# Pairwise products of 32 fields: cutting the first stores in fewer, larger pieces

One core of one Trainium2 chip; the metric is the device time of one execution in microseconds (us), median of several runs.

## The reference

```python
vid = jnp.einsum('bfd,de->bfe', x, W)          # x: (4096, 32, 64), W: (64, 64), float32
idx_i, idx_j = jnp.triu_indices(32, k=1)       # 496 pairs i < j
return x[:, idx_i, :] * vid[:, idx_j, :]       # (4096, 496, 64)
```

One small product with W, then 496 elementwise products per row of the batch. 34 MB come in and 520 MB go out: the output decides.

## The kernel before

The batch is cut into 16 tiles. In a tile the fields lie as `[128 partitions, field, 128]`, so a pair is 128 x 128 floats, 64 KB. TensorE makes `vid` in PSUM, VectorE multiplies into one of three output buffers of 124 pairs, SyncE issues the stores. From the third tile on there are four stores a tile, one of a whole buffer each (8.1 MB). In the first two tiles the buffers are sent in smaller pieces, so that the DMA engines have work before the first buffer is full; `GROWING` holds their sizes in pairs. The first two tiles of x are loaded on SyncE's queue, ahead of the stores; later ones on ScalarE's queue.

```python
GROWING = [21, 15, 19, 23, 27, 19, 29, ...]            # cut here: 26 sizes

loaded = [load(0, 4, nc.sync), load(1, 2, nc.sync)]    # 4 pieces, 2 pieces
...
for t in range(NT):
    if 0 < t < NT - 1:
        loaded.append(load(t + 1, 4, nc.scalar))
    ...                                                # matmuls of the tile
    for at, m, w, i, di, j, dj in products(by_field() if t < 2 else by_block()):
        base = at - at % SLOT                          # SLOT = 124
        if at == base:
            ot = opool.tile([P, SLOT, C], F32, tag="o", name=f"o_{t}_{at}")
        ...
        nc.vector.tensor_tensor(o, left, right, ALU.mult)
        at += n
        if t * NP + at == until or at in (base + SLOT, NP):
            nc.sync.dma_start(out=out[t][:, sent:at, :], in_=ot[:, sent - base : at - base, :])
            sent = at
            if t * NP + at == until:
                until += next(growing, NT * NP)
```

In the first two tiles the products come row by row: row j makes the j pairs (0, j) to (j-1, j). 21 pairs are the first six rows, 36 the first eight.

## Time and profile before

| | before |
|---|---|
| time, three runs | 1296.04 us (1294.44 to 1296.83) |
| profiled execution | 1297.8 us, span 1295.9 us |
| DMA engines | full in all of 40 slices but the last |
| VectorE busy | 1087.2 us, 84% |
| stores | 82, of them 26 cut by `GROWING` |

The lines are in the prediction below.

### The profile page before, as it was taken

Reading aid. Unit: us, or ns where it says so; the run is one execution under the profiler, and the core shown is the slowest. Engines: PE = TensorE matmul, PEld = TensorE weight load, DVE = VectorE, ACT = ScalarE, POOL = GpSimd, SP = SyncE. Lnnn points to the kernel's source line nnn. Section 1 sums busy time; section 2 is a strip of 40 time slices with the busy share of each in tenths; the row PEclk is TensorE's granted clock in tenths of the full one; section 3 lists DMA queues with packets and bytes.
Section 4 is the critical chain, followed back from the end, with each engine's and each line's share of the span. In section 5 each row is a group of like instructions: output and inputs, shape, how many; then the busy total and the mean of one; then the engine's idle time right before and its main releaser. Section 6 shows DMA issues by size and latency. Waiting matters only on the chain.

```text
span 1295.9 us, 1845 instructions
## 1 busy us (share of the span) xinstructions
PE 229.7 (18%) x512; PEld 48.5 (4%) x512; DVE 1087.2 (84%) x376; POOL 0.2 (0%) x4
## 2 busy tenths in 40 slices
PE   4112022112122121221212212122121221212000
PEld 1000000000000000000000000000000000000000
DVE  7999999788798887978879888798897978978870
POOL 0000000000000000000000000000000000000000
PEclk8555555555555555555655555555555555655555
DMA  9999999999999999999999999999999999999996
GB/s 390 431 422 439 427 431 450 432 423 439 430 434 429 425 438 434 424 432 429 435 432 432 433 433 433 434 432 433 435 432 432 431 432 432 430 431 445 437 425 276
DMA packets 20890, 553.80 MB, mean 427 GB/s; under 512 B 2448, under 2 KB 2448, under 8 KB 10256
## 3 DMA queue, kind: packets, MB, share of 16 engines
q1 hardware_dynamic: 12816, 524.33, 93.8%
q10 hardware_dynamic: 8064, 29.36, 5.5%
q8 instruction: 4, 0.07, 0.0%
q14 instruction: 6, 0.05, 0.0%
HBM read 33.59 MB, written 520.09 MB: 427 GB/s over the span
## 4 chain that ended last, share of the span: by engine, by line
DMA 55%; DVE 39%; issue 2%; PE 0%; DVEq 0%; SPq 0%
DMA out_dram<-o 55%; DVE o L159 39%; DMA x<-in_r_x_dram 0%; PE vid L134 0%; DVEq L200 0%; DVEq L159 0%; SPq L111 0%
## 5 line engine op out<-in xcount | busy, mean ns | idle before, releaser
L159 DVE TENSOR_TENSOR o<-x,vid 128x1024 f32<-128x1024 f32 (+15 forms) x376 | 1087.2, 2963 | 169.1 <-DMA out_dram<-o 124.3
L134 PE MATMUL vid<-x,w 64*64 64x512 f32 x512 | 229.7, 1032 | 958.6 <-DMA x<-in_r_x_dram 601.8
L134 PEld LDWEIGHTS vid<-x,w 64*64 64x64 f32 x512 | 48.5, 205 | 1138.1 <-DVE o L159 637.3
L182 POOL MEMSET const-uint8-127<- 128x1 uint8 x1 | 0.1, 103 | 0.0
L182 POOL MEMSET const-bfloat16-1.0<- 128x1 bf16 x1 | 0.1, 102 | 0.0
L182 POOL MEMSET const-float32-1.0<- 128x1 f32 x1 | 0.1, 100 | 0.0
L182 POOL MEMSET const-float32-0.0<- 128x1 f32 x1 | 0.1, 99 | 0.2 <-issue 0.2
## 6 DMA issues: line engine op xcount, KB each, us to landing
out_dram<-o SPq DMA_DIRECT2D x56, 7936.0 KB, 43.4
x<-in_r_x_dram ACTq DMA_DIRECT2D x56, 512.0 KB, 45.5
out_dram<-o SPq DMA_DIRECT2D x2, 3008.0 KB, 18.2
out_dram<-o SPq DMA_DIRECT2D x1, 5952.0 KB, 27.5
out_dram<-o SPq DMA_DIRECT2D x1, 4928.0 KB, 23.6
out_dram<-o SPq DMA_DIRECT2D x1, 4416.0 KB, 19.5
out_dram<-o SPq DMA_DIRECT2D x1, 4224.0 KB, 21.6
out_dram<-o SPq DMA_DIRECT2D x1, 3904.0 KB, 15.8
```

What stands on the lines that cost most here:

```text
L134: nc.tensor.matmul(vid[half, b : b + BANK, :], lhsT=w2[half, :], rhs=xt[half, b : b + BANK, :], start=True, stop=True,)
L159: nc.vector.tensor_tensor(o, left, right, ALU.mult)
L182: nc = _bacc.Bacc("TRN2", target_bir_lowering=False, num_devices=1, dynamic_dma_scratch_size=1024)
```

## The change

The intent is to issue the first store only when all first loads have landed, and to have fewer and larger stores behind it. Each further cut was chosen so that its store is ready before the stores ahead of it run out. Only the list changes.

```diff
 GROWING = [
-    21, 15, 19, 23, 27, 19, 29, 18, 19, 20, 38, 28, 24, 25, 47, 34, 29, 61,
-    55, 69, 66, 58, 77, 47, 93, 31,
+    36, 30, 25, 33, 29, 37, 41, 17, 52, 51, 21, 63, 61, 55, 69, 66, 58, 77,
+    47, 93, 31,
 ]
```

## The prediction

> **What bounds the kernel now.** I read the page first, from the span to the shares of the engines and the DMA rows.
>
> ```profile
> span 1295.9 us, 1845 instructions
> ...
> PE 229.7 (18%) x512; PEld 48.5 (4%) x512; DVE 1087.2 (84%) x376; POOL 0.2 (0%) x4
> ...
> DMA  9999999999999999999999999999999999999996
> ...
> q1 hardware_dynamic: 12816, 524.33, 93.8%
> q10 hardware_dynamic: 8064, 29.36, 5.5%
> ...
> HBM read 33.59 MB, written 520.09 MB: 427 GB/s over the span
> ```
>
> The DMA row is full in every slice but the last; VectorE, which makes the products, is idle for 16% of the span. The 16 DMA engines are the bound, and they are so from the first microseconds on. The reader should ask of any change here: does it take bytes away, does it make a byte cheaper, or does it open or close a hole in that row?
>
> Next I cut the span into stretches, to see the start, the growing stage, the steady part and the drain. The last two columns are the DMA share and the GB/s.
>
> ```profile
> 1.00:1.50 0.50, 0.00 (x0) 0.00 (x0) 0.00 (x0) 0.00 (x0) 1.00 0.00 0
> 1.50:2.00 0.50, 0.00 (x0) 0.00 (x0) 0.00 (x0) 0.00 (x0) 1.00 0.28 64
> ...
> 11.00:12.00 1.00, 1.00 (x8) 0.40 (x6) 1.00 (x2) 0.00 (x0) 1.00 1.05 442
> 12.00:13.00 1.00, 1.00 (x6) 0.30 (x4) 1.00 (x2) 0.00 (x0) 1.00 1.05 441
> 13.00:14.00 1.00, 1.00 (x8) 0.35 (x6) 1.00 (x1) 0.00 (x0) 1.00 0.98 414
> 14.00:15.00 1.00, 1.00 (x8) 0.25 (x4) 1.00 (x2) 0.00 (x0) 1.00 0.99 419
> 14.00:80.00 66.00, 12.34 (x32) 1.90 (x28) 66.00 (x33) 0.00 (x0) 0.56 1.02 431
> ...
> 300.00:1100.00 800.00, 145.56 (x314) 30.27 (x312) 673.09 (x215) 0.00 (x0) 0.53 1.00 432
> 1276.00:1280.00 4.00, 0.00 (x0) 0.00 (x0) 0.00 (x0) 0.00 (x0) 0.50 0.92 397
> 1280.00:1284.00 4.00, 0.00 (x0) 0.00 (x0) 0.00 (x0) 0.00 (x0) 0.50 0.62 270
> 1284.00:1288.00 4.00, 0.00 (x0) 0.00 (x0) 0.00 (x0) 0.00 (x0) 0.50 0.33 143
> 1288.00:1292.00 4.00, 0.00 (x0) 0.00 (x0) 0.00 (x0) 0.00 (x0) 0.50 0.04 16
> 1292.00:1296.00 4.00, 0.00 (x0) 0.00 (x0) 0.00 (x0) 0.00 (x0) 0.50 0.04 16
> ```
>
> Three things are to be seen. The hand-over from loads to stores (11 to 15 us) has no hole: 414 to 442 GB/s throughout. The growing stage (14 to 80 us) already runs at 431 GB/s against 432 in the steady part, so there is next to nothing to win in it. And the end is not a common one: the rate falls by steps for some 12 us, to 16 GB/s, less than one engine's share of 432/16 = 27. The last-finishing DMA engine sets the end; the others are done earlier. The whole then adds up: the full-rate body is 553.8 MB / 432 GB/s = 1282 us, the loss before the first packets is about 2.5 us, and the drain loses (4 us x 5) - (397+270+143+16+16) x 4 / 432 = 12.2 us; the sum, 1296.7, is the span to 1 us.
>
> Last, the queue that issues the stores, and the VectorE instruction that finishes pair 36 (start, length):
>
> ```profile
> 0.73 0.38 SPq L111 DMA_DIRECT2D w<-in_L_rec_W_dram  x1
> 1.17 3.12 SPq L117 DMA_DIRECT2D x<-in_r_x_dram  x6
> 10.89 0.35 SPq L162 DMA_DIRECT2D out_dram<-o  x1
> ...
> 13.02 0.34 SPq L162 DMA_DIRECT2D out_dram<-o  x1
> ...
> 11.78 1.22 DVE L159 TENSOR_TENSOR o<-x,vid 128x1024 f32<-128x1024 f32 x1
> ```
>
> The first store (21 pairs) is issued at 10.89, while the DMA engines still work through the loads. The second (up to pair 36) follows the eighth row of products, which ends at 11.78 + 1.22 = 13.00.
>
> **What the Trainium skill says.** Page "DMA: Bandwidth & Descriptors", section "Queues, rings and completion order": on each DMA engine the descriptors of one queue are consumed in ring order. First loads and stores share SyncE's queue, so a store issued before the loads are through is simply queued behind them and starts without a hole; the unbroken GB/s from 11 to 15 us agree. Same page, "Latency and other measured facts": about 600 ns to the first byte of a DMA issued by SyncE. The trace agrees if counted from the end of the issuing instruction: the issue of w ends at 0.73 + 0.38 = 1.11, nothing moves to 1.50, and in still finer stretches the first packets start between 1.70 and 1.80, some 0.63 us after it and 1.0 us after the issue began. Same page, "Anatomy of one DMA": a fixed cost of about 2 us per DMA, most of it the write receipt at completion. That would make five DMAs fewer worth 10 us if it lay on the path; the trace says it does not, since 431 GB/s with many small stores against 432 with large ones leaves at most 66 us x 1/432 = 0.15 us (rounding of the rates: up to 0.3) for all of the stores in that stage.
>
> **The change part by part.** It touches only where stores are cut: 26 sizes become 21, the first 36 instead of 21. Bytes, products, matmuls and their order are untouched; the built programs show 82 stores before and 77 after, and both lists meet again at pair 496 (the end of the first of 16 tiles), so everything from the second tile on is the same.
>
> Removed: five stores. In packets: each store is 128 rows and 16 completion packets, since (82 stores + 6 loads + 1 load of w) x 144 = 12816, the count of q1. So a store is 8 rows and one small packet per DMA engine. What a packet costs beyond its bytes I estimate from the two queue rows: q10 took 5.5% of 16 x 1295.9 us = 1140 us for 7168 packets of 4 KB, 159 ns each; q1 took 93.8% = 19449 us for 524.33 MB, 37.1 ns per KB, at a mean of some 46 KB per data packet. At q1's rate 4096 bytes would take 152 ns, so about 8 ns are left per packet, give or take 1.5 for the rounding of 5.5%. Per store 9 x 8 = 72 ns on each engine, all engines alongside; five stores: 0.36 us less.
>
> Added: a hole. The first store now waits for pair 36, so it is issued at 13.02, not 10.89; its first packets come 1.0 us later, about 14.05. When do the engines run out of loads? The six loads and w are 4.23 MB. From the rates of the first microseconds (about 3.4 MB moved by 10.9 us), 0.85 MB were left, or 2.0 us at 430 GB/s: 12.85 us in the mean, with some engines half a microsecond earlier and later. So each DMA engine idles 0.7 to 1.4 us, 1.15 in the mean, and since the DMA is the bound this is not earned back.
>
> Moved: the later stores. For no further hole, each must be issued 1.0 us before the stores ahead of it run out. One pair is 64 KB, 0.152 us at 430 GB/s, and the queue starts at 14.05. Store 2 (to pair 66) is ready when the eleventh row is, about 17.2, so its packets can come at 18.2; store 1 lasts to 14.05 + 36 x 0.152 = 19.5: 1.3 us to spare. The same sum for the others, with VectorE's times from the trace: to pair 91, 21.7 against 24.1; to 124, 26.3 against 27.9; to 153, 30.3 against 32.9; to 190, 35.4 against 37.3; to 231, 41.0 against 42.9; to 300, 50.4 against 51.8; to 351, 57.4 against 59.7; to 435, 68.8 against 70.6; to 496, 77.1 against 80.2. None is late, and a later start would only add room. VectorE's own pace, 0.133 us a pair and some 0.15 us an instruction, does not depend on the stores until its buffers come round again.
>
> Sum: +1.15 - 0.36 = +0.8 us, on 1296.04: 1296.8 us.
>
> **The rivals.** First, a gain: fewer, larger stores lift the growing stage by more than the packet sum. For it stands only the skill's fixed cost; against it the 431 GB/s. If the first store's early packets also disturbed the last loads, they would have to show as a dip at 11 to 13 us, and there is none. At its best this rival makes 1295.5 us. Second, a hidden hole: the last-finishing engine sets the end, and it might be one of those whose loads end late, so that its own hole is only 0.6 us; with the 0.36 saved the time is then 1296.3, the same as before. Third, a longer hole: the first loads needed until about 4 us to reach full rate after packets first moved at 2.2, so engines may start the store staggered. Stores read SBUF and not HBM, and w's packets all start within 0.3 us, which speaks against it; if it came, the hole would be near 2 us and the time 1297.8. Fourth, a new starvation at the tightest of the later stores (to pairs 66 and 300, 1.3 us to spare): each miss would add some tenths of a us, no more than 1 in all. Fifth, the drain: the spread of 12 us between DMA engines builds up over the long steady part, and a shift of the start may move it by a microsecond either way.
>
> **Range and chances.** The three runs of before spread over 2.4 us, more than the effect. From 1296.8, with a us for the drain and a us for the state of the run to both sides: 1294.8 to 1299.0. Two per cent would be 26 us; no part of this change touches even 3 us. Faster 0.005, within 2% 0.99, slower 0.005.
>
> **What would show it right or wrong.** In the changed kernel the one store issue at 13.02 must be the first; the stretch 13 to 14 us must fall far under 400 GB/s (to 100 or less) and 14 to 15 be full again; the stretch 15 to 80 should stay at 430 or more, which shows no later starvation; the steady part must keep 432, and the drain its 12 us. Wrong would be: no hole at 13 to 14 us (then a store starts faster than w did), a second hole later on, or a steady rate above 432, which would mean that the cuts of the first tile matter for the rest.

## The result, and the profile after

The changed kernel took 1301.14 us (median of 4 runs, 1300.61 to 1301.38), the kernel before, beside it, 1295.24 us (1293.92 to 1296.83). The ratio is 1.0044, with a 95% interval of 1.0027 to 1.0062; ratios here are the mean time of one kernel's runs over that of the other's of the same rounds, so not quite the ratio of the medians. It is outside the predicted range: 1296.8 us was said, 1299.0 at most.

The page of the changed kernel shows the same picture at its top, a little longer.

```profile
span 1298.7 us, 1833 instructions
...
PE 229.5 (18%) x512; PEld 48.6 (4%) x512; DVE 1087.3 (84%) x376; POOL 0.2 (0%) x4
...
q1 hardware_dynamic: 12096, 524.33, 93.5%
...
HBM read 33.59 MB, written 520.09 MB: 426 GB/s over the span
```

VectorE's work and all bytes are the same; q1 (SyncE's queue) has 720 packets fewer, which are the five stores at 144 packets. The stretches that the prediction asked for (columns: stretch and its length, busy time of the four engines, clock, DMA share, GB/s):

```profile
11.00:12.00 1.00, 1.00 (x6) 0.30 (x4) 1.00 (x2) 0.00 (x0) 1.00 1.06 451
12.00:13.00 1.00, 1.00 (x8) 0.43 (x6) 1.00 (x2) 0.00 (x0) 1.00 0.71 295
13.00:14.00 1.00, 1.00 (x8) 0.33 (x6) 1.00 (x2) 0.00 (x0) 1.00 0.02 8
14.00:15.00 1.00, 1.00 (x6) 0.30 (x4) 1.00 (x2) 0.00 (x0) 1.00 0.99 424
15.00:80.00 65.00, 12.42 (x32) 1.96 (x28) 65.00 (x32) 0.00 (x0) 0.54 1.02 432
...
300.00:1100.00 800.00, 146.38 (x318) 30.50 (x314) 674.17 (x217) 0.00 (x0) 0.53 1.00 433
1276.00:1280.00 4.00, 0.00 (x0) 0.00 (x0) 0.00 (x0) 0.00 (x0) 0.50 1.13 492
1280.00:1284.00 4.00, 0.00 (x0) 0.00 (x0) 0.00 (x0) 0.00 (x0) 0.50 0.84 365
1284.00:1288.00 4.00, 0.00 (x0) 0.00 (x0) 0.00 (x0) 0.00 (x0) 0.50 0.33 143
1288.00:1292.00 4.00, 0.00 (x0) 0.00 (x0) 0.00 (x0) 0.00 (x0) 0.50 0.07 32
1292.00:1296.00 4.00, 0.00 (x0) 0.00 (x0) 0.00 (x0) 0.00 (x0) 0.50 0.07 32
```

The hole is there, 8 GB/s from 13 to 14 us, and full rate right after it. No second hole follows (432 GB/s from 15 to 80 us), and the steady rate is unchanged. The first store and the row it waits for:

```profile
12.18 1.21 DVE L159 TENSOR_TENSOR o<-x,vid 128x1024 f32<-128x1024 f32 x1
...
13.42 0.35 SPq L162 DMA_DIRECT2D out_dram<-o  x1
```

It was issued at 13.42 and not at 13.02, since VectorE had waited longer for the matmuls: 0.62 us before its fourth row, against 0.23. That is scatter between executions and not the change: in a second trace of the kernel before the fourth row is late in the same way, and in neither trace of it does this open a hole.

So far the prediction holds. The two spans differ by 2.8 us; the medians of the timed runs by 5.9. The trace of before that I worked from was one of the slow executions of a kernel that scatters. What scatters is the drain, the time at the end in which one DMA engine after another runs out of work, and the trace lets us take it apart: each DMA engine closes its part of the last store with one packet of 4 bytes, so the start times of the last 16 such packets say when each of the 16 engines was done. This was worked out from the DMA packets of the traces (us after the first engine):

```
before, run of 1297.8 us: 0.0 0.0 0.1 0.2 0.2 0.2 0.3 0.3 1.8 2.1 3.2 5.1 6.6 7.1 7.2 12.5   first at 1282.20
before, run of 1291.9 us: 0.0 0.2 0.2 0.2 0.2 1.0 1.5 1.6 1.8 2.1 2.4 2.6 4.6 5.4 5.7  6.6   first at 1282.24
after,  run of 1300.6 us: 0.0 0.1 0.1 0.1 0.1 0.2 0.2 0.6 1.6 2.0 4.1 4.1 4.3 5.2 8.9 13.7   first at 1283.61
```

The mean engine of before is done at 1285.1 and 1284.5 us, that of after at 1286.4: a steady difference of some 1.6 us. The slowest is 9.6 and 4.3 us behind the mean before, and 10.9 after; this lag of the slowest engine, and its growth in the run, are called drift below. The kernel ends with the slowest. The question for the experiments was why the slowest engine falls so far behind after the change.

### The profile page after: what moved, and what is told of

Read it like the earlier page. It is cut to its first block, busy times and chain, and to the rows that moved or that the text cites. A ratio compares the mean times of both kernels' runs of the same rounds, so it can differ in the third digit from the quotient of the medians.

```text
span 1298.7 us, 1833 instructions
## 1 busy us (share of the span) xinstructions
PE 229.5 (18%) x512; PEld 48.6 (4%) x512; DVE 1087.3 (84%) x376; POOL 0.2 (0%) x4
## 4 chain that ended last, share of the span: by engine, by line
DMA 60%; DVE 36%; issue 1%; PE 0%; DVEq 0%; SPq 0%; ACTq 0%
DMA out_dram<-o 58%; DVE o L159 36%; DMA x<-in_r_x_dram 2%; PE vid L134 0%; DVEq L200 0%; DVEq L159 0%; SPq L111 0%; ACTq L117 0%; SPq L162 0%
```

## The experiments

Each batch ran on one chip with its own 11 runs of the kernel before; the kernels themselves ran six times, those of eight loads four and five; all results were correct. "Mean" is when the 16 DMA engines were done on average in the profiled execution, "behind" how much later the slowest was; the time of a run is the slowest engine's end plus 3.0 to 3.3 us.

| run | median us | range us | ratio to before | run traced | mean | behind |
|---|---|---|---|---|---|---|
| c_before | 1294.16 | 1291.92 to 1298.71 | 1.0000 | 1291.92 | 1284.5 | 4.3 |
| c_after | 1300.99 | 1300.29 to 1301.70 | 1.0045 | 1300.59 | 1286.5 | 10.8 |
| e_first36 | 1299.48 | 1299.16 to 1300.41 | 1.0035 | 1299.44 | 1286.3 | 10.1 |
| e_few_no_hole | 1295.95 | 1295.38 to 1296.65 | 1.0007 | 1295.91 | 1285.0 | 7.7 |
| e_first28 | 1300.47 | 1300.03 to 1301.11 | 1.0055 | 1300.74 | 1286.3 | 11.2 |
| e_first55 | 1301.78 | 1300.92 to 1302.68 | 1.0063 | 1302.68 | 1288.8 | 10.7 |
| e_late_hole | 1300.38 | 1299.96 to 1301.49 | 1.0045 | 1300.91 | 1287.3 | 10.6 |
| e_fill | 1298.83 | 1295.86 to 1301.17 | 1.0042 | 1295.86 | 1286.3 | 6.3 |
| e_fill_again | 1298.52 | 1296.61 to 1299.29 | 1.0027 | 1299.21 | 1286.8 | 9.2 |
| e_before_fill | 1300.38 | 1296.47 to 1300.65 | 1.0040 | 1298.93 | 1286.9 | 8.9 |
| e_before_stagger | 1294.36 | 1291.79 to 1297.78 | 0.9999 | 1294.09 | 1285.4 | 5.6 |
| e_stagger | 1300.51 | 1296.62 to 1302.47 | 1.0051 | 1301.88 | 1288.9 | 9.8 |
| e_oneq_before | 1298.65 | 1295.90 to 1302.55 | 1.0028 | 1299.25 | 1287.8 | 8.4 |
| e_oneq_after | 1301.82 | 1298.34 to 1303.11 | 1.0042 | 1298.34 | 1288.5 | 6.5 |
| e_oneq_first55 | 1305.13 | 1303.67 to 1307.25 | 1.0075 | 1307.25 | 1292.8 | 11.3 |
| e_load1 | 1303.34 | 1299.46 to 1308.25 | 1.0061 | 1303.69 | 1288.7 | 12.0 |
| e_load8_before | 1325.10 | 1324.90 to 1325.58 | 1.0235 | 1324.90 | 1320.7 | 1.2 |
| e_load8_after | 1322.85 | 1322.14 to 1325.57 | 1.0223 | 1322.85 | 1318.2 | 1.4 |

**Both kernels again.** No edit.

> The kernel before, unchanged, for a second trace and for the noise. Both theories: ratio 1.000 within 0.001, times of 1293 to 1298 us. The spread between the first and the last DMA engine at the end was some 12 us in the first trace, which was one of its slower executions (1297.8 us); if the drain explains the run-to-run range, a trace of a 1295 us execution should show some 3 us less of it.

> The changed kernel, unchanged, for a second trace. Again 1300.6 to 1301.4 us, ratio 1.0044. Theory 'hole': the engines idle some 1.5 us near 13 us and the rest of the 5.9 us is a longer drain. Theory 'chance': the time falls back to some 1297.5 us when it is run again.

The second trace of before caught a fast execution. Its drain (the same stretches; from 1280 us on):

```profile
1280.00:1284.00 4.00, 0.00 (x0) 0.00 (x0) 0.00 (x0) 0.00 (x0) 0.50 0.66 286
1284.00:1288.00 4.00, 0.00 (x0) 0.00 (x0) 0.00 (x0) 0.00 (x0) 0.50 0.18 79
1288.00:1292.00 4.00, 0.00 (x0) 0.00 (x0) 0.00 (x0) 0.00 (x0) 0.50 0.00 0
```

In the first trace 143 and 16 GB/s stood where here are 79 and 0: the slowest engine was done 6 us sooner (1288.83 against 1294.72), the mean one only 0.6, and the runs differ by 5.9 us. So the scatter of before is the slowest engine's. The changed kernel hardly scatters (1.4 us in six runs) and is always at the slow end. The theory "chance" falls.

**Which part of the change.** One kernel takes only the late first store, the other only the larger cuts behind it:

```diff
-    21, 15, 19, 23, 27, ...
+    36, 19, 23, 27, ...                # e_first36: the rest as before
+    21, 15, 30, 25, 33, 29, ...        # e_few_no_hole: the rest as after
```

> First store of 36 pairs, all other cuts as before: 25 growing stores. If the late first store is the cause: as the changed kernel, ratio 1.004 (1300 to 1301.5 us). If the fewer and larger stores after it are the cause: as before or a little more, ratio 1.0005 to 1.0015.

> First stores of 21 and 15 pairs as before, then the changed kernel's larger cuts: 22 growing stores and no hole. If the late first store is the cause: as before, less the 0.3 us of the four stores saved, ratio 0.9995 to 1.000. If the cuts are the cause: ratio 1.003 to 1.0045.

The late first store alone costs 0.35% (1.0035) of the change's 0.45%; the larger cuts alone make 1.0007, whose interval (0.9982 to 1.0033) includes 1. So within the change the late first store is the cause. Five stores fewer gain nothing that can be seen.

**Its size.** The first theory I then tried was "phase". The loads leave the 16 engines 0.8 to 1.1 us apart; behind the hole their first store packets all start within 0.15 us of one another. The theory says that engines in step lose more later.

```diff
-    36, 30, 25, 33, ...
+    28, 38, 25, 33, ...                # e_first28
+    55, 36, 33, ...                    # e_first55
```

> First store of 28 pairs, ready some 1.1 us before that of 36: its packets can come at about 13.0 us, when half of the DMA engines still work on the loads. The hole is 0.1 to 0.2 us in the mean, and the stagger shrinks to 0.3 to 0.5 us. Theory 'phase': between the two kernels, 1295.5 to 1299 us, drain 9 to 12 us. Theory 'hole alone': as before less the stores saved, 1293.5 to 1295 us.

> First store of 55 pairs, ready 2.7 us later than that of 36. Theory 'phase': the engines are in step as in the changed kernel, and only the hole grows: 1301.0 + 2.7 = 1303.7 us, drain 13 to 14 us. Theory 'hole alone', with 6 us lost for a hole of 1.5 us: in proportion, some 1312 us.

e_first28 was ill made: with a first store that short the second, of 38 pairs, came too late, and the hole had only moved.

```profile
13.00:14.00 1.00, 1.00 (x8) 0.34 (x6) 1.00 (x2) 0.00 (x0) 1.00 1.13 477
14.00:15.00 1.00, 1.00 (x6) 0.30 (x4) 1.00 (x2) 0.00 (x0) 1.00 0.94 387
17.00:18.00 1.00, 0.20 (x2) 0.20 (x4) 1.00 (x2) 0.00 (x0) 1.00 0.55 229
18.00:19.00 1.00, 0.88 (x4) 0.00 (x0) 1.00 (x1) 0.00 (x0) 1.00 0.73 311
```

477 and 387 GB/s where the hole was, 229 and 311 a little later. Its 1300.5 us, as the changed kernel's, are then no surprise, and it tells nothing about a smaller hole. e_first55 has no DMA traffic from 14 to 17 us; its first store was issued at 16.32, 2.9 us after the changed kernel's, and its mean engine ended 2.3 us later. But its slowest was no further behind (10.7 us), and the runs were only 0.7 us longer by the medians, 2.3 by the ratios. The extra cost is not in proportion to the hole: it is there at 1.3 us and does not grow with 4.

**A hole elsewhere.** The early stores of before, but a hole at the end of the first tile:

```diff
-    ..., 47, 34, 29, 61, 55, ...
+    ..., 47, 34, 90, 55, ...           # e_late_hole
```

> The kernel before, early stores as they were, but the stores of 29 and 61 pairs at the end of the first tile are one of 90: it is ready at 76.0 us and the queue runs dry at some 75.5, so the hole of 1.5 us lies there and not at the first store. Theory 'phase' (any hole puts the engines into step, and in step the slowest one always drifts far): as the changed kernel, the mean DMA engine ends 1.5 us later than before, the slowest 10 to 11 us behind the mean, 1299.5 to 1301.5 us, runs within 2 us of each other. If the hole only adds its own length: 1295.5 to 1297 us. If it is the loads beside the first store that matter: as before, 1294 to 1296 us.

```profile
74.00:75.00 1.00, 0.00 (x0) 0.00 (x0) 1.00 (x1) 0.00 (x0) 0.50 0.90 383
75.00:76.00 1.00, 0.00 (x0) 0.00 (x0) 1.00 (x1) 0.00 (x0) 0.50 0.09 35
76.00:77.00 1.00, 0.41 (x2) 0.29 (x4) 1.00 (x4) 0.00 (x0) 0.50 0.00 0
77.00:78.00 1.00, 1.00 (x4) 0.00 (x0) 1.00 (x3) 0.00 (x0) 0.50 1.90 737
...
1284.00:1288.00 4.00, 0.00 (x0) 0.00 (x0) 0.00 (x0) 0.00 (x0) 0.50 0.33 143
1288.00:1292.00 4.00, 0.00 (x0) 0.00 (x0) 0.00 (x0) 0.00 (x0) 0.50 0.22 95
1292.00:1296.00 4.00, 0.00 (x0) 0.00 (x0) 0.00 (x0) 0.00 (x0) 0.50 0.07 32
```

The hole lies at 75 to 77 us, 2.1 us for each engine in place of the expected 1.5, and the result is the changed kernel's in all respects: 1300.4 us, 1.5 us of scatter, the slowest 10.6 us behind. So neither the first loads nor the first store as such matter. "Phase" had said just this.

**The delay without the hole.** The decisive test of "phase": the stores come as late, but the DMA engines are kept busy in between by loads that nobody uses. They then go into the stores one after another, as the loads left them. The same was done with the kernel before.

```diff
 loaded = [load(0, 4, nc.sync), load(1, 2, nc.sync)]
+filler = opool.tile([P, SLOT, C], F32, tag="o", name="filler")
+nc.sync.dma_start(out=filler[:, 0:12, :], in_=x[1][:, 20:32, :])
```

> The changed kernel, with its hole filled: behind the loads 12 more fields (0.79 MB, 1.8 us at 430 GB/s) are loaded into an output buffer not yet in use. The DMA engines then never stop before the first store and keep the stagger (0.8 us between the first and the last) with which the loads leave them. Theory 'phase' (the hole puts the 16 engines into step, and engines in step lose more time later, so the drain grows): the loss is only the 1.8 us of extra bytes less 0.4 us of saved stores, median 1295 to 1297 us, with the scatter of the kernel before. Theory 'hole alone' (idle time or late stores as such cost 6 us, whatever the phase): as the changed kernel, 1300.5 to 1302 us.

> The changed kernel with its hole filled by more loads, a second time, since its six runs spread over 5 us and fell between the theories (1298.8). Pure 'phase': median 1295 to 1297; if it is 1298 to 1300 again, the stagger at the start explains the scatter but not all of the mean.

> The kernel before with all its cuts, and 12 fields (0.79 MB, 1.8 us) loaded into an unused output buffer between the loads and the first store: no hole, stagger kept, but all stores 1.8 us later against VectorE. If only a hole makes the large drift: the mean engine ends 1.8 us later, the slowest 4 to 10 us behind it as before, median 1295.5 to 1297. If a later stream of stores by itself raises the drift (as the two fillings of the changed kernel, 1298.5 and 1298.8, suggest): 1298 to 1299.5.

```profile
12.00:13.00 1.00, 1.00 (x8) 0.30 (x4) 1.00 (x2) 0.00 (x0) 1.00 0.98 403
13.00:14.00 1.00, 1.00 (x7) 0.31 (x5) 1.00 (x2) 0.00 (x0) 1.00 1.01 363
14.00:15.00 1.00, 1.00 (x8) 0.44 (x6) 1.00 (x2) 0.00 (x0) 1.00 0.95 319
15.00:16.00 1.00, 1.00 (x8) 0.15 (x2) 1.00 (x1) 0.00 (x0) 1.00 1.11 465
...
1284.00:1288.00 4.00, 0.00 (x0) 0.00 (x0) 0.00 (x0) 0.00 (x0) 0.50 0.37 159
1288.00:1292.00 4.00, 0.00 (x0) 0.00 (x0) 0.00 (x0) 0.00 (x0) 0.50 0.22 95
1292.00:1296.00 4.00, 0.00 (x0) 0.00 (x0) 0.00 (x0) 0.00 (x0) 0.50 0.04 16
```

This is the kernel before with its loads lengthened: the DMA share stays at 0.95 to 1.11 from 12 to 16 us, there is no hole, and the engines are 1.0 us apart all through the first tile. And yet it takes 1300.4 us, 6 us more than before, for 1.8 us of bytes. With the changed kernel's cuts the same loads make 1298.8 and 1298.5 us. "Phase" had allowed 1295 to 1297 in all three and falls as the explanation of the mean. What is common to all the slow ones so far is only that the stores run later against VectorE and the loads, by 1.1 us or more; a hole is one way to get there. What remains of "phase" is the scatter: nearly all two-queue kernels whose engines go into step early scatter by 1 to 2 us, and those that start staggered by 3 to 7 us. That is a pattern across these runs and not a proof. The difference in the stagger itself is also short-lived: behind the first loads of the second queue, at 90 to 95 us, the engines are 0.8 to 1.4 us apart in all of the traces so far, in step before or not.

**The stagger itself.** Small loads to some of the rows only, to set the engines further apart: in the changed kernel behind its first store, in the kernel before ahead of it.

```diff
+for s in range(7):                                    # e_stagger, behind the first store of after
+    k = 14 - 2 * s
+    nc.sync.dma_start(out=filler[:k, 6 * s : 6 * s + 6, :], in_=x[1][:k, 0:6, :])
+for s, k in enumerate((13, 10, 8, 5, 2)):             # e_before_stagger, behind the loads of before
+    nc.sync.dma_start(out=filler[:k, 8 * s : 8 * s + 8, :], in_=x[1][:k, 0:8, :])
```

> The changed kernel with its hole left in, but right after the first store seven small loads go to 14, 12, 10, 8, 6, 4 and 2 of the DMA engines, 3 KB a row, so that the engines are some 0.8 us apart again from the second store on. Theory 'phase': although bytes are added, the drain is back to 6 to 12 us in place of 13.6, median 1295 to 1299 us. Theory 'hole alone': 1301 to 1302 us.

> The kernel before with five small loads of 4 KB rows to 13, 10, 8, 5 and 2 of the DMA engines between the loads and the first store, so that the engines start the stores up to 0.8 us further apart, without a hole. If a wider stagger means less drift: 1289 to 1293 us, better than before. If the drift of before is not set by the width of the stagger: 1294 to 1296.5 us, with its scatter of several us.

A DMA of 128 rows leaves 16 completion packets, one for each engine. The five small loads add 76 packets to q1, which are 38 rows and 38 completions: each reached as many engines as it has rows. e_stagger failed by its own fault: in the program every DMA waits for the one eight issues before it, so with seven loads between the second store waited for the first one to land, was issued at 21.5 us in place of 17.6, and left a second hole. e_before_stagger was sound: its engines ended the first two stores 2.3 us apart, in place of 0.8 in the traces of before, and it made 0.9999. A wider stagger at the start does not help.

**Where the engines lose the time.** In the traces the spread between first and last engine grows, with pauses, from 80 us to 1180 us, and stands still after that (12.5 us at 1189 us and at the end in the first trace of before). Nor does it grow from 16 to 79 us (0.8 and 0.6 us in that trace), when there are no loads either: it grows while loads of x run and not when there are only stores. In the first traces of before and after, seven or eight of the 16 engines stay within 0.3 us of one another to the end; the others leave this pack one by one. Two tests of the loads: on the stores' own queue, and in other sizes.

```diff
-            loaded.append(load(t + 1, 4, nc.scalar))
+            loaded.append(load(t + 1, 4, nc.sync))     # e_oneq_before, e_oneq_after, e_oneq_first55
+            loaded.append(load(t + 1, 1, nc.scalar))   # e_load1
+            loaded.append(load(t + 1, 8, nc.scalar))   # e_load8_before, e_load8_after
```

> The kernel before, but the later loads of x are issued on the queue of the stores and not on ScalarE's. In the traces so far the DMA engines drift apart only while loads and stores share an engine from two queues, and not in the last 100 us, where there are no loads. Theory 'two queues make the drift': the drain falls from 6 to 15 us to 2 us at most, the run-to-run scatter to under 1.5 us, and the time to 1284 to 1288 us. Theory 'the drift is made by the stores or by the engines themselves': 1292 to 1298 us as before.

> The changed kernel, with the same one queue. If the two-queue drift is gone, what is left of the change is its hole (1.5 us) less the five stores (0.4 us): 1.0 to 1.5 us more than the kernel before with one queue, where the two-queue pair differs by 6 us. If the change costs 6 us by another way than the drift, the pair differs by 5 to 7 us here too.

> First store of 55 pairs, one queue. A hole simply adds: 2.3 to 2.8 us more than the changed kernel with one queue, 3.5 to 4.2 more than the kernel before with one queue.

> The kernel before, each later x loaded by one DMA of 16 KB rows in place of four of 4 KB rows, still on ScalarE's queue: 8 load packets on each DMA engine a tile in place of 32. Theory 'two queues make the drift', with each mixing of a load packet into a store losing a little: the drain falls to a third or so, 1286 to 1290 us. If the number of load packets does not matter: 1290 to 1299 us as before.

> The kernel before, each later x loaded by eight DMAs of 2 KB rows in place of four of 4 KB. Theory 'each mixing of a load packet into a store can cost its engine up to a load packet's time' (16 KB rows made the slowest engine 12 us later than the mean, 4 KB rows 4 to 10): the mean DMA engine ends some 4 us later (448 packets more at 8 to 9 ns), but the slowest ends only 3 to 5 us behind the mean: 1292 to 1295 us, runs within 4 us. If the length of the load packet does not matter: 1298 us.

> The changed kernel with eight loads of 2 KB rows. With the drift halved, the changed kernel's extra drift is halved too: 2.5 to 4 us more than the kernel before with the same loads, in place of 6. If the change's extra time does not come from the drift, it stays 6 us.

My theory that two queues make the drift fell: with one queue the slowest engine is still 6.5 to 11.3 us behind. But the traces show where the time goes. With two queues, store packets of 63,488 bytes take 2.342 us each, but a few hundred of the 7168 take more; the sum of the excess over all 16 engines is 34 us and 22 us in the two traces of before, 33 and 32 in those of after, some two thirds of it in the last packet of a store, and nothing after 1200 us. The load packets have 1.5 to 1.9 us of excess. With one queue it is the other way round: 8 to 9 us in the stores (24 in e_oneq_first55), 49 to 54 in the later load packets. So some engines lose time wherever loads are mixed with stores; that the loss falls on whichever packet is under way is my reading and not tested. The sum does not tell the slow kernels from the fast: e_first36, 10.1 us behind, has 25 us of excess in its stores, and e_few_no_hole, 7.7 us behind, 31. What differs is how much of it falls on one engine. One load of 16 KB rows in place of four of 4 KB makes it worse (91 us of excess, slowest 12 us behind).

With one queue the late store costs 3.2 us and not 6 (1301.8 against 1298.7, with ranges that overlap), and e_oneq_first55 3.3 more; by the means of the six runs it is 1.8 and 4.2. The mean engine ends 0.7 and 5.0 us later than in e_oneq_before. So the pair lies between the two theories that I had written down (1.0 to 1.5, or 5 to 7 us), and these runs do not decide between them.

The loads of eight pieces broke something else. Every DMA waits for the one eight issues before it, as in e_stagger. With four loads and four stores a tile that is the same piece of the tile before; with eight loads a tile, each of its four stores comes eight issues after a load. What SyncE waited for before it issued the stores, first in the kernel before, then in e_load8_before (us in total, times, longest), with a stretch of the latter:

```profile
SPq L162 <- DVE o L159: 1167.3, 80, 20.7
SPq L162 <- DMA x<-in_r_x_dram: 51.5, 5, 18.0
```

```profile
SPq L162 <- DMA x<-in_r_x_dram: 526.8, 46, 22.7
SPq L162 <- DMA out_dram<-o: 501.0, 13, 44.1
SPq L162 <- DVE o L159: 219.6, 33, 25.3
...
70.00:74.00 4.00, 0.00 (x0) 0.00 (x0) 4.00 (x2) 0.00 (x0) 0.50 0.00 0
```

In the kernel before the stores waited for VectorE, here for other DMAs. The queue of stores ran dry again and again, at first for some 8 us from 70 us on, and a run took 1325 us. That its slowest engine is only 1.2 us behind says little then: an engine that is ahead stands still until the next store is issued, and so I take it that the late ones catch up at each dry stretch. e_load8_after was 2.3 us faster than e_load8_before (1322.85 against 1325.10, with ranges that overlap), where 2.5 to 6 us more had been expected. The test of the load's length failed.

No experiment was faster than the kernel before beyond the noise.

## Why the prediction was wrong

**The bound, the hole and the later cuts were right.** The hole was put at 1.15 us. Between the mean end of the loads on an engine and the start of its first store packet there were 1.42, 1.29 and 1.14 us in the traces of after, c_after and e_first36, although the store was issued at 13.42 to 13.52 and not at 13.02. That is partly luck: in the same traces the loads ended at 12.90, 13.14 and 13.27 us in the mean, and not at 12.85, which made up for some of it. None of the later stores was late: in the two traces of the changed kernel the engines show no idle time from 14.6 to 80 us.

**The saved stores** were put at 0.36 us; e_few_no_hole, with four fewer, is 1.0007. The gain is not seen, and it is too small for these runs to deny it. The fixed cost of 2 us that the prediction takes from the skill is one that its section gives for DMAs issued from GpSimd, as its heading says; these stores are issued by SyncE.

**The sum** of the two, +0.8 us, describes the mean DMA engine: 1286.4 and 1286.5 against 1285.1 and 1284.5, some 1.7 us. It is more than 0.8 in part because the hole was longer than 1.15 us, and in part because the mean engine shares in the drift of the next point (the excess of its store packets is 34/16 = 2.1 and 22/16 = 1.4 us before, 2.1 after).

**The step that failed** is the fifth rival, in its words "a shift of the start may move it by a microsecond either way", and with it the range. I had read correctly that the last-finishing engine sets the end, and had then treated its lag as a constant with a little noise. It is the largest term. Medians less 3.1 (before) or 3.3 us (after), and less the mean engine's end, give 1294.2 - 3.1 - 1284.8 = 6.3 us behind the mean for before and 1301.0 - 3.3 - 1286.5 = 11.2 for after: 4.9 of the 6.8 us between these medians. A later position of the stores, by 1.1 us or more, brings this lag to 9 to 11 us in nearly all traces, whether by a hole at the start, a hole at 76 us, or busy engines with no hole at all; with busy engines single runs still came out low (e_fill's traced run of 1295.86 us has 6.3).

A second fault went into it: the one trace that I had of before was a slow execution (9.6 us behind), so nothing in it showed that the lag is mostly smaller. That the profiled run was slower than all timed ones, by 1 to 3 us, was on the page of times and should have made me ask what scatters.

**What stays open** is why a shift of little more than 1 us sets the lag. The lag grows over 1100 us while loads and stores are mixed, long after VectorE has come to follow the stores; phase explains at most the scatter, and the second queue not even that (e_oneq_before scatters by 6.7 us). In the changed kernel the drift hardly varies: with the 16 engines in the order of their ends, its two traces differ by at most 1.3 us (the slowest by less than 0.1), those of before by up to 5.9. I have no theory that the runs do not contradict.

## What to carry to other kernels

Where static shares of the work lie on 16 DMA engines, the time is that of the slowest: take the end apart by engine before you call the bound a mean rate, and take two traces if the profiled run is not near the median. A queue that is always full at the start is worth having even with small stores: here the first store issued 2.5 us later (13.42 against 10.89) cost 6 us, and five stores fewer gained nothing measurable. And an experiment that keeps the engines busy for the same time as a hole is what separates "idle" from "late".

## What the Trainium skill lacked or had wrong

- "DMA: Bandwidth & Descriptors" gives no figure for how far the 16 engines drift apart in a long stream of equal shares (a row of its table names two engines as usually slower; these traces do not number the engines): here 4 to 11 us between the mean and the slowest after 1290 us, growing only while loads and stores are mixed.
- The same page, "Rules for kernel authors", asks for large transfers (1 MiB and more per DMA). Here one load of 2 MB in place of four of 512 KB was slower than before (1.0061, interval 1.0040 to 1.0081), with the slowest engine 12 us behind.
- The same page, "Anatomy of one DMA", puts about 2 us of fixed cost on a DMA, by its heading one issued from GpSimd; the section has no such figure for DMAs issued from SyncE. Here, for SyncE's stores behind a full queue, none of it shows: four times 2 us would have made some 0.994 (an estimate from that figure), and four stores fewer made 1.0007 (0.9982 to 1.0033).
